# Four fused blocks on one core: a quad's reciprocal and scaling written behind the mask addition of the quad two further on

## The chip, the core and the metric

The kernel runs on one core of a Trainium2 chip. Its time is the device time of one execution in microseconds, the median of several runs; lower is better. The engines are called by the profile's names: PE (TensorE, matmuls), PEld (its weight loads), DVE (VectorE), ACT (ScalarE), POOL (GpSimd) and SP (SyncE, which issues nearly all DMAs). All arithmetic is float32.

## What is computed

An image batch `x` of 4 x 56 x 56 x 256 goes through four residual blocks, each `x = x + block(groupnorm(x))`:

- layer 0: attention in a 7 x 7 window around every pixel, 8 heads of 32 channels, keys and values padded with zeros at the border
- layer 1: every image's 3136 tokens against each other: `A = exp(5 * cosine)` without its diagonal, normalised by rows, then `rowsum * (xW + b) - (A x) W`, layer norm, leaky ReLU
- layer 2: neighbourhood attention with a 7 x 7 window clamped at the border and a position bias; half of the heads use a dilation of 2
- layer 3: attention inside shifted 7 x 7 windows, with a position bias and a mask

The part that the change touches is the softmax of layers 0, 2 and 3, cut to its core:

```python
logits = q @ k + bias_or_mask
attn = softmax(logits)              # exp(l) / sum(exp(l))
out = attn @ v                      # here: (exp(l) @ v) * (1 / sum(exp(l)))
x = x + out @ w_o + b_o
```

## The kernel before, in words

`direct_blocks` computes everything without subtracting a maximum before the exponential. At its end a flag tells whether any sum became too large; only then a second program, `fused_blocks`, computes all again. It did not run here.

In layers 0, 2 and 3 the work is a stream of **quads**. A quad is four heads times one tile of queries (112 in layer 0, 98 in layer 2, four pairs of windows of 98 in layer 3) with all keys that these queries see. Two quads (eight heads) make up a tile in layers 0 and 2, and a row of windows in layer 3. There are 224, 256 and 64 quads.

`attend_quads` (L932) runs the stream. For each quad:

1. `logits` (L941): PE multiplies keys by queries (L948) into two PSUM tiles of two banks, `s0` and `s1`, one buffer each. For the first half DVE adds the mask into SBUF tile `e0` (L954) and ACT takes the exponential in place (L955). For the second half ACT takes the exponential straight from PSUM (L957) and POOL multiplies by the exponential of the mask (L958).
2. `fill`: the steps of other work dealt out to this quad by `spread`: projections of the next rows (L901 with their evictions by ACT, values at L918 with L920 on DVE), the output projection of the row before (L901 on `attn`), normalisation (L895), statistics (L872), loads.
3. `products` of the quad before this one (`held`): PE multiplies the exponentials by the values and by ones (L967) into `ps_o`: numerators and sums. Then its `done` step: in layers 0 and 2 after every second quad, in layer 3 after each, `finish` takes the reciprocal of the sums into tile `rs` (L1091 or L1093 and L1096 in layer 0, L1416 in layer 2, L1633 in layer 3), POOL adds `rs` to a running sum (`seen`, L926), and DVE scales the numerators into `attn` (L1098, L1422, L1635). That makes 112 + 128 + 64 = 304 finishes.

`ps_o` has two buffers in layers 0 and 2 (one for a pair of quads) and a single one of two banks in layer 3. The output projection of row r - 1 reads `attn` and is dealt out within row r: in layer 3 it is the first step of the second quad's fill.

What decides the order on an engine: the Python source records operations in the order in which it runs. The framework then builds one list per engine. It takes an operation when the operations that it needs are ready by its own reckoning and its buffers are free, and among those that are ready it takes the one recorded first. Semaphore waits are put in afterwards. The built list of an engine can so differ from the source. In DVE's list of the kernel before, 277 of the 304 finishes have the mask addition of the quad two further on between reciprocal and scaling, although the source has it behind both.

Of the kernel before, what the change touches and what calls it, by code (L numbers as in the profile page):

```python
# [814 lines left out]
def direct_blocks(ctx: ExitStack, tc: tile.TileContext, d: dict, watch):  # L815
# [7 lines left out]
    no_step = lambda: None  # L823
# [27 lines left out]
    def psum_tile(tag, bufs, banks=1):  # L851
        shape = [P, 512] if banks == 1 else [P, banks, 512]
        return ps.tile(shape, FP, tag=tag, name="ps_" + tag, bufs=bufs)
# [78 lines left out]
    def attend_quads(pool, units):  # L932

        def logits(w):  # L941
            nk, nq, nu = w["nk"], w["nq"], len(w["pieces"])
            w["first"]()
            w["e"] = []
            s = [psum_tile(f"s{a}", 1, 2) for a in range(2)]
            for u, (k, q, *_) in enumerate(w["pieces"]):
                for j in range(4):
                    nc.tensor.matmul(s[j // 2][:nk, j % 2, u * nq:(u + 1) * nq], lhsT=k(j), rhs=q(j),  # L948
                                     start=True, stop=True)
            for a in range(2):  # L950
                e = pool.tile([P, 2, w["width"]], FP, tag=f"e{a}", name=f"e{a}", bufs=2)
                ev, sv = e[:nk, :, :nu * nq], s[a][:nk, :, :nu * nq]
                if a == 0:
                    nc.vector.tensor_tensor(ev, sv, w["mask"].to_broadcast([nk, 2, nu * nq]), ALU.add)  # L954
                    nc.scalar.activation(ev, ev, AF.Exp)  # L955
                else:
                    nc.scalar.activation(ev, sv, AF.Exp, accum_out=w.get("sum"))  # L957
                    nc.gpsimd.tensor_tensor(ev, ev, w["emask"].to_broadcast([nk, 2, nu * nq]), ALU.mult)  # L958
                w["e"].append(e)

        def products(w):
            nk, nq = w["nk"], w["nq"]
            for k in range(2):
                for u, (_, _, v, start, stop) in enumerate(w["pieces"]):
                    po = w["o"](k, u)
                    for j in range(4):
                        nc.tensor.matmul(  # L967
                            po[j * HD:(j + 1) * HD], lhsT=ones[:nk, :HD] if k else v(j),
                            rhs=w["e"][j // 2][:nk, j % 2, u * nq:(u + 1) * nq], start=start, stop=stop)
            w["done"]()  # L970

        held = None
        for w in units:
            logits(w)
            w["fill"]()
            if held:
                products(held)
            held = w
        products(held)

    def spread(units, steps):

        n = len(units)
        for i, w in enumerate(units):
            mine = steps[i * len(steps) // n:(i + 1) * len(steps) // n]
            w["fill"] = lambda mine=mine: [f() for f in mine]
            yield w
# [11 lines left out]
    def layer0(big, pool):  # L999
# [151 lines left out]
        for r in range(3):  # L1151
            prepare(r)
            if r < 2:
                for step in project_rows(r):
                    step()
        attend_quads(pool, stream())
        for step in project_out(NIMG * NCH - 1):
            step()
# [186 lines left out]
    def layer2(big, pool):  # L1345
# [153 lines left out]
        for i in range(3):  # L1499
            prepare(i + 1)  # L1500
            for step in project_rows(i):
                step()
        attend_quads(pool, stream())
        for step in project_out(NIMG * NSB - 1):
            step()
# [61 lines left out]
    def layer3(big, pool):  # L1567
# [108 lines left out]
        for step in project_rows(0):  # L1676
            step()
        attend_quads(pool, stream())
        for step in project_out(NIMG * 8 - 1):
            step()  # L1680
# [74 lines left out]
def _build(arrays):  # L1755
    import concourse.bacc as bacc

    nc = bacc.Bacc("TRN2", target_bir_lowering=False, num_devices=1)
    d = {n: nc.dram_tensor("in_" + n, a.shape, mybir.dt.from_np(a.dtype), kind="ExternalInput").ap()
         for n, a in arrays.items()}  # L1760
    d["out"] = nc.dram_tensor("out_x", (NIMG, C, T), FP, kind="ExternalOutput").ap()
    with tile.TileContext(nc) as tc:
        with tc.tile_pool(name="flag", bufs=1) as pool:
            flag = pool.tile([1, 1], I32, name="flag")
            with tc.tile_pool(name="watch", bufs=1) as wp:
                watch = [wp.tile([P, n], FP, name=f"watch{n}") for n in (WC, 2 * CC + 2, 4 * NIMG * 8)]
                for w in watch:
                    nc.vector.memset(w, 0.0)
                direct_blocks(tc, d, watch)
                unsafe(tc, wp, watch, flag)  # L1770
            again = nc.values_load(flag)
            with tc.If(again > 0):
                fused_blocks(tc, d)
    return nc
# [10 lines left out]
```

## Time and profile before

| what | value |
|---|---|
| median of 3 runs | 4694.75 us (4692.59 to 4698.1) |
| the profiled execution, as a run | 4702.85 us |
| its span, first to last instruction | 4701.1 us |
| mean granted PE clock | 0.973 |
| DVE: reciprocals L1416, L1633, L1096, L1091 busy | 176.5, 166.5, 111.5, 62.2 us |
| mean of one of them | 1379, 2602, 1549, 1556 ns |
| DVE: mask addition L954, layers 0, 2, 3 busy | 152.1, 146.2, 58.6 us |
| mean of one of them | 679, 571, 915 ns |
| DVE: scaling L1422, L1098, L1635 busy | 52.7, 42.6, 35.4 us |

The profile is of one execution. Times are counted from the span's start. A row of the timeline has the start, the busy time, the engine, the line, the operation with its output and inputs and how many were merged, and in brackets how long the engine sat idle before it and what ended that. A row of busy time by stretch has the stretch and its length, then the busy time and count of PE, PEld, DVE, ACT and POOL, the granted PE clock, the DMA engines' busy share and GB/s. A row of the waits has who waited for whom, the total in microseconds, how often, and the longest.

Layer 0 takes roughly the stretch from 65 to 935 us, layer 1 from 935 to 3150, layer 2 from 3150 to 4000 and layer 3 from 4000 to the end. The change does not touch layer 1.

### The profile page before, as it was taken

Reading aid. Unit: us, or ns where it says so; the run is one execution under the profiler, and the core shown is the slowest. Engines: PE = TensorE matmul, PEld = TensorE weight load, DVE = VectorE, ACT = ScalarE, POOL = GpSimd, SP = SyncE. Lnnn points to the kernel's source line nnn. Section 1 sums busy time; section 2 is a strip of 40 time slices with the busy share of each in tenths; the row PEclk is TensorE's granted clock in tenths of the full one; section 3 lists DMA queues with packets and bytes.
Section 4 is the critical chain, followed back from the end, with each engine's and each line's share of the span. In section 5 each row is a group of like instructions: output and inputs, shape, how many; then the busy total and the mean of one; then the engine's idle time right before and its main releaser. Section 6 shows DMA issues by size and latency. Waiting matters only on the chain.

```text
span 4701.1 us, 104255 instructions
## 1 busy us (share of the span) xinstructions
PE 4340.8 (92%) x44910; PEld 2896.0 (62%) x44910; DVE 2384.5 (51%) x4745; ACT 1369.8 (29%) x2750; POOL 1458.5 (31%) x1835
## 2 busy tenths in 40 slices
PE   6989999899999999999999999969999998888887
PEld 4756666566665666666666666646666665555554
DVE  5566666633444333443434433445666666555655
ACT  2234444411111111111111111114444444333332
POOL 2234444411124111231123211224344444333333
PEclk9799999999999999999999999989999999999999
DMA  5243333210000000010000000033333333211211
GB/s 196 72 123 105 118 102 94 86 40 9 22 17 25 13 20 15 17 33 8 22 13 17 16 8 9 16 113 90 101 99 98 100 100 113 63 56 55 61 56 43
DMA packets 237208, 277.91 MB, mean 59 GB/s; under 512 B 20270, under 2 KB 229088, under 8 KB 236000
## 3 DMA queue, kind: packets, MB, share of 16 engines
q1 hardware_dynamic: 236306, 270.30, 18.8%
q8 instruction: 354, 5.80, 0.5%
q14 instruction: 116, 0.95, 0.1%
q10 hardware_dynamic: 432, 0.86, 0.0%
HBM read 191.58 MB, written 79.53 MB: 58 GB/s over the span
## 4 chain that ended last, share of the span: by engine, by line
PE 72%; DVE 12%; POOL 6%; issue 5%; DMA 3%; ACT 1%; SPq 0%; DVEq 0%; POOLq 0%; ACTq 0%
PE ps_m L901 14%; PE ps_o L1266 11%; PE ps_o L967 9%; PE ps_s L1231 9%; PE ps_v L1258 9%; PE ps_m L918 7%; PE ps_s L948 5%; PE ps_t L1249 2%; DVE e L954 2%; POOL y L1299 2%; POOL y L1300 2%; PE ps_m L1204 2%; DMA x<-in_x 1%; DVE xn L895 1%; POOL rstd L1297 1%
## 5 line engine op out<-in xcount | busy, mean ns | idle before, releaser
L1262 DVE TENSOR_TENSOR acc<-acc,ps_v 128x257 f32<-128x257 f32 x1104 | 458.3, 420 | 773.8 <-PE ps_v L1258 769.8
L1266 PE MATMUL ps_o<-xw,at 128*128 128x257 f32 (+1 forms) x2400 | 664.9, 394 | 1.1 <-DVE at L908 0.8
L1234 ACT ACTIVATE e<-ps_s 128x512 f32<-128x512 f32 (+5 forms) x364 | 195.3, 537 | 1592.4 <-PE ps_s L1231 1559.8
L1258 PE MATMUL ps_v<-xw,e 128*128 128x257 f32 (+1 forms) x2400 | 647.4, 385 | 6.2 <-DVE acc L1260 6.2
L1231 PE MATMUL ps_s<-xnT,xd 128*128 128x512 f32 (+4 forms) x1456 | 628.2, 546 | 0.0
L957 ACT ACTIVATE e<-ps_s 119x392 f32<-119x392 f32 (+7 forms) x544 | 324.6, 597 | 754.8 <-PE ps_s L948 738.6
L1266 PEld LDWEIGHTS ps_o<-xw,at 128*128 128x128 f32 (+1 forms) x2400 | 422.0, 189 | 165.7 <-ACT at L910 56.8
L926 POOL TENSOR_TENSOR watch<-watch,rs 128x196 f32<-128x196 f32 (+2 forms) x304 | 215.7, 710 | 985.8 <-DVE rs L1633 396.3
L1258 PEld LDWEIGHTS ps_v<-xw,e 128*128 128x128 f32 (+1 forms) x2400 | 407.4, 186 | 105.8 <-DVE acc L1262 31.1
L955 ACT ACTIVATE e<-e 119x392 f32<-119x392 f32 (+7 forms) x544 | 343.1, 631 | 418.7 <-DVE e L954 404.6
L901 PE MATMUL ps_m<-xn,w_wqkv 128*128 128x392 f32 x1024 | 395.4, 518 | 30.5 <-DVE xn L895 30.5
L1227 POOL TENSOR_SCALAR xd<-xnT,vec 128x128 f32<-128x128 f32 (+1 forms) x200 | 121.5, 619 | 851.6 <-PE ps_s L1231 842.3
L958 POOL TENSOR_TENSOR e<-e,m0t 119x448 f32<-119x448 f32 (+3 forms) x224 | 294.9, 1317 | 227.5 <-ACT e L957 226.7
L967 PE MATMUL ps_o<-e,ones 100*32 100x112 f32 (+7 forms) x10752 | 360.4, 256 | 0.0
L1231 PEld LDWEIGHTS ps_s<-xnT,xd 128*128 128x128 f32 x1456 | 254.3, 189 | 167.2 <-issue 149.1
L967 PEld LDWEIGHTS ps_o<-e,vp 119*32 119x32 f32 (+4 forms) x8704 | 193.3, 111 | 237.9 <-issue 159.2
L958 POOL TENSOR_TENSOR e<-e,bias 119x392 f32<-119x392 f32 (+3 forms) x256 | 259.1, 1012 | 232.6 <-ACT e L957 232.3
L918 PE MATMUL ps_m<-w_wqkv,xn 128*98 128x256 f32 x1024 | 259.4, 398 | 65.2 <-ACT k L1610 41.6
L967 PE MATMUL ps_o<-e,vp 119*32 119x98 f32 (+6 forms) x8704 | 310.8, 263 | 4.8 <-POOL e L958 4.1
L920 DVE TENSOR_TENSOR v<-ps_m,bc 98x512 f32<-98x512 f32 (+1 forms) x184 | 126.4, 687 | 359.5 <-PE ps_m L918 246.9
L967 PEld LDWEIGHTS ps_o<-e,ones 100*32 100x32 f32 (+5 forms) x10752 | 278.4, 112 | 7.3 <-issue 7.3
L901 PEld LDWEIGHTS ps_m<-xn,w_wqkv 128*128 128x128 f32 x1024 | 184.1, 193 | 142.6 <-issue 20.7
(137 smaller groups left out, 5932.1 us busy)
## 6 DMA issues: line engine op xcount, KB each, us to landing
x<-in_x SPq DMA_DIRECT2D x56, 448.0 KB
x<-xr SPq DMA_DIRECT2D x56, 448.0 KB
x<-x SPq DMA_DIRECT2D x60, 392.0 KB
xr<-x SPq DMA_DIRECT2D x60, 392.0 KB
vp<-vd SPq DMA_DIRECT2D x224, 59.5 KB
xr<-in_x SPq DMA_DIRECT2D x28, 448.0 KB
vd<-v SPq DMA_DIRECT2D x28, 448.0 KB
xr<-x SPq DMA_DIRECT2D x28, 448.0 KB
```

The costliest lines, as they stand in the source:

```text
L901: nc.tensor.matmul(pm[:, :n], lhsT=w[:, h, col:col + P], rhs=rhs(h), start=(h == 0), stop=(h == CC - 1))
L918: nc.tensor.matmul(pm[:n, j * C:(j + 1) * C], lhsT=xn[:, h, k * n:(k + 1) * n], rhs=w[:, h, :], start=(h == 0), stop=(h == CC - 1))
L926: nc.gpsimd.tensor_tensor(w, w, rs, ALU.add)
L948: nc.tensor.matmul(s[j // 2][:nk, j % 2, u * nq:(u + 1) * nq], lhsT=k(j), rhs=q(j), start=True, stop=True)
L955: nc.scalar.activation(ev, ev, AF.Exp)
L957: nc.scalar.activation(ev, sv, AF.Exp, accum_out=w.get("sum"))
L958: nc.gpsimd.tensor_tensor(ev, ev, w["emask"].to_broadcast([nk, 2, nu * nq]), ALU.mult)
L967: nc.tensor.matmul(po[j * HD:(j + 1) * HD], lhsT=ones[:nk, :HD] if k else v(j), rhs=w["e"][j // 2][:nk, j % 2, u * nq:(u + 1) * nq], start ...
L1231: nc.tensor.matmul(s[:nj, :n], lhsT=xd[j][:, h, :nj], rhs=xnT[:, h, first * P:first * P + n], start=(h == 0), stop=(h == CC - 1))
L1258: nc.tensor.matmul(pv[:ni, :C + 1], lhsT=e[:nj, col(i)], rhs=xw[:nj, j, :], start=True, stop=True)
L1262: nc.vector.tensor_tensor(acc[:ni, i, :], acc[:ni, i, :], pv[:ni, :C + 1], ALU.add)
L1266: nc.tensor.matmul(out[j][:nj, :C + 1], lhsT=e[:nj, col(i)] if i == j else at[:size(i), tcol(i)], rhs=xw[:size(i), i, :], start=(i == j), ...
```

## The change

The `done` step of a quad is no longer called at the end of `products`. The loop keeps it and calls it in the next turn, behind `logits` of the next quad in line and ahead of that quad's fill. After the last quad the two steps still open are called. Nothing else changes: no operation, no buffer and no shape. From the first changed line on, lines of the kernel after are numbered 1 higher (inside `logits` and `products`) or 4 higher (below the loop).

```diff
@@ -967,16 +968,19 @@
                         nc.tensor.matmul(
                             po[j * HD:(j + 1) * HD], lhsT=ones[:nk, :HD] if k else v(j),
                             rhs=w["e"][j // 2][:nk, j % 2, u * nq:(u + 1) * nq], start=start, stop=stop)
-            w["done"]()
-
-        held = None
+
+        held, done = None, no_step
         for w in units:
             logits(w)
+            done()
             w["fill"]()
             if held:
                 products(held)
+                done = held["done"]
             held = w
+        done()
         products(held)
+        held["done"]()
```

## The prediction

> **What bounds the kernel now.** I read the page first, then busy time by stretch, then the waits, then the timeline at the places that the change reaches. The page:
>
> ```profile
> PE 4340.8 (92%) x44910; PEld 2896.0 (62%) x44910; DVE 2384.5 (51%) x4745; ACT 1369.8 (29%) x2750; POOL 1458.5 (31%) x1835
> ...
> PE 72%; DVE 12%; POOL 6%; issue 5%; DMA 3%; ACT 1%; SPq 0%; DVEq 0%; POOLq 0%; ACTq 0%
> ```
>
> TensorE is busy or first in the chain nearly everywhere; VectorE (DVE), which the change re-sorts, has 12% of the chain. Busy time by stretch; the three rows are layers 0, 2 and 3:
>
> ```profile
> 65.00:935.00 870.00, 827.48 (x13906) 558.59 (x13902) 551.34 (x826) 366.27 (x710) 366.04 (x341) 0.94 0.33 98
> ...
> 3150.00:4000.00 850.00, 807.47 (x14730) 532.73 (x14729) 510.70 (x927) 381.59 (x832) 334.29 (x392) 0.98 0.34 101
> 4000.00:4701.10 701.10, 588.07 (x7437) 375.06 (x7436) 387.51 (x528) 219.24 (x384) 263.74 (x326) 0.97 0.18 54
> ```
>
> PE (first figure after the length) is idle 42.5, 42.5 and 113.0 us. In layer 3 the waits give part of it to the step that the change wants ahead:
>
> ```profile
> PE ps_s L948 <- DVE e L954: 38.0, 31, 1.2
> ```
>
> So logits wait 38.0 us for the previous mask addition (L954) to free the score buffer; the same line reads 26.7 in layer 0 and 10.9 in layer 2. The reason seems to be the reciprocal ahead of it. An ordinary layer 3 row:
>
> ```profile
> 4208.34 0.95 PE L948 MATMUL ps_s<-q,k 32*98 32x98 f32 x32
> 4208.55 2.61 DVE L1633 RECIPROCAL rs<-ps_o 128x392 f32<-128x392 f32 x1
> ...
> 4211.07 0.91 DVE L954 TENSOR_TENSOR e<-ps_s,m3l 98x784 f32<-98x784 f32 x1
> ...
> 4211.90 0.55 DVE L1635 SCALAR_TENSOR_TENSOR attn<-ps_o,rs 128x392 f32<-128x392 f32 x1
> ...
> 4212.52 1.58 PE L901 MATMUL ps_m<-attn,w_wp 128*128 128x392 f32 x4
> ```
>
> The source of before writes reciprocal, scaling, mask addition. The chip ran reciprocal, **mask addition**, scaling. The list is sorted by readiness, and source order only breaks ties.
>
> **What the Trainium skill says.** "PSUM — Partial Sum Buffer", section "Engine vs sequencer instructions": VectorE, ScalarE and GpSimd work strictly first in, first out, and matmuls start and complete in program order. So what counts is the built list, not the source. The trace agrees: at 4211.07 the mask addition starts 1.78 us after its logits ended (4209.29), behind the reciprocal. "VectorE: DVE Perf Modes", section "First, the fixed hardware budget": a reciprocal is an iterative division with a repeat count of 8. The trace agrees that it is dear: 2.61 us against 0.55 for the scaling of the same 128x392. This is what a mask addition would be spared.
>
> **The change, part by part.** It adds and removes no arithmetic, so its price is in order, waits and addresses. I compared the built lists of both kernels, engine by engine, line numbers shifted to match.
>
> 1. VectorE: 304 pairs of reciprocal and scaling (112 + 128 + 64). Before, in 277 the mask addition stands between the two (91, 127, 59), in 27 none does. After, 281 have it between (92, 127, 62). In none does it stand ahead of the reciprocal, in either kernel. So the list differs in four swaps of neighbours: one in layer 0, three in layer 3, once at the start of images 1 to 3.
> 2. TensorE: four matmuls (eight passes) of the products move ahead of a value projection at those three places; nothing else. ScalarE: at the same places the exponential (L955) moves ahead of the key eviction (L1610).
> 3. GpSimd and SP: same operations in the same order, so every DMA is issued from its old place. In layer 3 the rs and xr tiles get swapped addresses.
>
> The layer 3 place, seen at image 1:
>
> ```profile
> 4150.57 0.94 PE L948 MATMUL ps_s<-q,k 32*98 32x98 f32 x30
> ...
> 4153.29 3.81 DVE L895 TENSOR_SCALAR xn<-x,gst 128x343 f32<-128x343 f32 x6
> ...
> 4156.47 5.56 PE L901 MATMUL ps_m<-xn,w_wqkv 128*128 128x392 f32 x8 [4.96 <-DVE xn L895]
> 4157.02 0.55 DVE L1635 SCALAR_TENSOR_TENSOR attn<-ps_o,rs 128x392 f32<-128x392 f32 x1
> ...
> 4157.51 0.96 DVE L954 TENSOR_TENSOR e<-ps_s,m3l 98x784 f32<-98x784 f32 x1
> ...
> 4160.76 0.59 ACT L1610 ACTIVATE k<-ps_m,vec 128x392 f32<-128x392 f32 x1 [8.20 <-PE ps_m L901]
> 4161.25 0.85 ACT L955 ACTIVATE e<-e 98x784 f32<-98x784 f32 x1
> 4161.96 0.51 PE L967 MATMUL ps_o<-e,v 98*32 98x98 f32 x2
> ```
>
> What is late is the normalisation; PE waits 4.96 us for it, and the swap stands behind it. Swapped, the mask addition starts at 4157.02, 0.49 earlier, and ends near 4157.93; the scaling then ends near 4157.93 + 0.55 + 0.08 = 4158.6, some 1.0 later. The scaling's reader is the first product (the output buffer is single in layer 3), at 4161.96: 3.4 us of cover, given by eight key and query matmuls. Without that cover it would cost 1.0. The exponential gets idle ScalarE time near 4158 (its 8.20 idle) and stops standing between two evictions. PE waited 0.26 for L955 before the value projection; the four products moved there fill that. Gain 0 to 0.26 at each of three, none if the clock or the next eviction takes it: 0 to -0.8. Against: if the cover failed everywhere, 3 x 1.0 = +3.0.
>
> Layer 0's place:
>
> ```profile
> 256.83 0.63 DVE L872 BATCH_NORM_STATS2 st<-x 128x6 f32<-128x448 f32 x1 [5.69 <-DMA x<-in_x]
> 257.37 0.38 DVE L1098 TENSOR_TENSOR attn<-ps_o,rs 128x224 f32<-128x224 f32 x1
> 257.66 0.85 DVE L954 TENSOR_TENSOR e<-ps_s,m0t 100x672 f32<-100x672 f32 x1
> ...
> 258.57 1.15 PE L948 MATMUL ps_s<-q,kE 32*119 32x112 f32 x16 [3.87 <-DVE e L954]
> ```
>
> PE stood still for this mask addition, itself behind a statistic that waits for a DMA. Swapped it starts 0.29 earlier, and so do the logits: 0 to -0.3. The low end counts because the chain goes back to the next x<-in_x transfer 1.4 us later, which does not move. The scaling's reader is an output projection several quads on.
>
> Addresses: both rs buffers are used in turn already, and the 64 reciprocals in layer 3 span only 2587 to 2609 ns, their 64 GpSimd readers 1010 to 1039. If every one went to its extreme it would be 64 x 0.03 = 2 us, on engines with slack; I take 0.
>
> Sum: bounds -1.1 and +3.0; I take -0.5. The profiled execution spans 4701.1 us (4702.85 as a run), so its like would span 4700.6. That run lies 8.1 us above the median of three, 4694.75, from which I forecast 4694.3.
>
> **Rivals.**
> - A, faster: the mask addition really goes ahead of the reciprocal. Then at most the PE waits of layers 0 and 2 vanish, 26.7 + 10.9 = 37.6 us: 4657. For it: those waits and the row above. Against: the list has no such case.
> - B, slower: the same in layer 3, where the scaling is the next thing needed. Mask addition 4209.29 to 4210.20, reciprocal to 4212.81, scaling to 4213.44; the output projection that now starts at 4212.52 would start 0.9 later. In 31 rows: +28 us, 4723. It decides from about ten rows on (10 x 0.9 = 9). Against it: the list again, and the earlier release of the scores.
> - C: the change does not do what it says. That is my forecast: four swaps of 304.
> - D: the cover of step 1 fails, +3.0: 4698, still no difference.
>
> **How the numbers follow.** About 0.2%, 9.4 us, is what a measurement of this kernel can tell from no change. Forecast, C: 0.91, with D's 0.04 inside "same"; A 0.02; B 0.03. Range: the three runs span 5.5 us and another median may sit as far off: 4694.3 - 5.5 = 4688.8, and with D above, 4694.3 + 5.5 + 3.0 = 4702.8, about where the profiled run lies. I write 4688.5 to 4702.5. A and B stay outside, with 0.05.
>
> **What would show it.** Right: layers 0, 2 and 3 as long as before within 2 us each; L954 still between L1633 and L1635 in ordinary rows; the 38.0 us wait still there; at the start of images 1 to 3 L954 ahead of L1635 and L955 ahead of L1610, with PE's 4.96 unchanged. Wrong: L954 ahead of L1633 (A, B), L901 waiting longer for L1635 (B), or products waiting for L1635 at those three places (D). Also wrong: a shift in all layers, which no part here can make.

## The result, and the profile after

The changed kernel takes 4698.55 us (median of 4 runs, 4692.99 to 4703.24), beside 4696.43 us of the kernel before on the same chip (4 runs, 4692.59 to 4702.7). The ratio is 1.0003, with a 95% interval of 0.9985 to 1.002: no difference. The profiled execution spans 4697.9 us (4699.74 as a run); that of before spanned 4701.1.

The page of the kernel after, busy time and the chain's shares by engine:

```profile
PE 4334.9 (92%) x44910; PEld 2891.5 (62%) x44910; DVE 2383.9 (51%) x4745; ACT 1371.5 (29%) x2750; POOL 1460.8 (31%) x1835
...
PE 72%; DVE 12%; POOL 6%; issue 5%; DMA 3%; ACT 1%; SPq 0%; DVEq 0%; POOLq 0%; ACTq 0%
```

The same instructions, the same shares, digit for digit in the chain. Measured from the last output addition of one layer to that of the next (layer 3 then begins at 3980.8 us and not at the rough 4000 of the table of stretches), layers 0 to 3 took 933.6, 2189.4, 857.8 and 720.3 us before, and 932.3, 2187.9, 857.5 and 720.2 after. Layer 1, which has no part in the change, moved by 1.5 us; that is as much as any.

The waits of the kernel after from 4000 us to the end (who waited for whom, total us, how often, longest):

```profile
PE ps_m L918 <- ACT k L1614: 41.6, 28, 2.4
PE ps_s L949 <- DVE e L955: 38.0, 31, 1.2
```

The 38.0 us of logits waiting for the mask addition are untouched. The 41.6 us above it, which the prediction did not look at, become the subject of the experiments. An ordinary layer 3 row of the timeline of after:

```profile
4163.62 0.95 PE L949 MATMUL ps_s<-q,k 32*98 32x98 f32 x32
4163.75 2.61 DVE L1637 RECIPROCAL rs<-ps_o 128x392 f32<-128x392 f32 x1
...
4166.27 0.91 DVE L955 TENSOR_TENSOR e<-ps_s,m3l 98x784 f32<-98x784 f32 x1
...
4167.10 0.55 DVE L1639 SCALAR_TENSOR_TENSOR attn<-ps_o,rs 128x392 f32<-128x392 f32 x1
```

Reciprocal, mask addition, scaling: the order of before. The edit is in the source and not in the list. The start of image 1, one of the three places in layer 3 where the list does differ:

```profile
4154.32 4.38 PE L901 MATMUL ps_m<-xn,w_wqkv 128*128 128x392 f32 x8 [4.96 <-DVE xn L895]
...
4154.88 0.96 DVE L955 TENSOR_TENSOR e<-ps_s,m3l 98x784 f32<-98x784 f32 x1
...
4155.76 0.55 DVE L1639 SCALAR_TENSOR_TENSOR attn<-ps_o,rs 128x392 f32<-128x392 f32 x1
4155.87 0.86 ACT L956 ACTIVATE e<-e 98x784 f32<-98x784 f32 x1 [5.45 <-DVE e L955]
...
4158.08 0.59 ACT L1614 ACTIVATE k<-ps_m,vec 128x392 f32<-128x392 f32 x1 [1.35 <-PE ps_m L901]
...
4158.63 0.53 PE L968 MATMUL ps_o<-e,v 98*32 98x98 f32 x10
```

Mask addition ahead of scaling, exponential ahead of key eviction, and the first products 2.3 us behind the scaling's end, with no wait for it. Below, a *pass* is one PE instruction of the profile; the eight passes (x8) at 4154.32 are the key and query matmuls. From their start, the mask addition comes at 0.56 (1.04 before), the scaling at 1.44 (0.55 before).

### The profile page after: what moved, and what is told of

Its sections match the earlier page's. It is cut to its first block, busy times and chain, and to the rows that moved or that the text cites. A ratio compares the mean times of both kernels' runs of the same rounds, so it can differ in the third digit from the quotient of the medians.

```text
span 4697.9 us, 104254 instructions
## 1 busy us (share of the span) xinstructions
PE 4334.9 (92%) x44910; PEld 2891.5 (62%) x44910; DVE 2383.9 (51%) x4745; ACT 1371.5 (29%) x2750; POOL 1460.8 (31%) x1835
## 4 chain that ended last, share of the span: by engine, by line
PE 72%; DVE 12%; POOL 6%; issue 5%; DMA 3%; ACT 1%; SPq 0%; DVEq 0%; POOLq 0%; ACTq 0%
PE ps_m L901 14%; PE ps_o L1270 11%; PE ps_s L1235 9%; PE ps_o L968 9%; PE ps_v L1262 9%; PE ps_m L918 7%; PE ps_s L949 5%; PE ps_t L1253 2%; DVE e L955 2%; DMA x<-in_x 2%; POOL y L1303 2%; POOL y L1304 2%; PE ps_m L1208 2%; DVE xn L895 1%; POOL rstd L1301 1%
## 5 line engine op out<-in xcount | busy, mean ns | idle before, releaser
L1270 PEld LDWEIGHTS ps_o<-xw,at 128*128 128x128 f32 (+1 forms) x2400 | 422.0, 189 | 165.6 <-ACT at L910 56.7
L918 PE MATMUL ps_m<-w_wqkv,xn 128*98 128x256 f32 x1024 | 257.5, 396 | 65.3 <-ACT k L1614 41.6
```

Of the source, the lines that this page charges most:

```text
L918: nc.tensor.matmul(pm[:n, j * C:(j + 1) * C], lhsT=xn[:, h, k * n:(k + 1) * n], rhs=w[:, h, :], start=(h == 0), stop=(h == CC - 1))
L1270: nc.tensor.matmul(out[j][:nj, :C + 1], lhsT=e[:nj, col(i)] if i == j else at[:size(i), tcol(i)], rhs=xw[:size(i), i, :], start=(i == j), ...
```

## The experiments

Every difference below is against the kernel before, run on the same chip: its median is 4697.76 us beside the first four kernels, 4694.37 beside `late_projection`, `mask_02_scale_3`, `late_projection_mask_3` and `late_mask_02_scale_3`, and 4697.11 beside the other four. A ratio and its interval rest on all runs, so a ratio can differ a little from the quotient of two medians. Lengths of layers, waits, idle and busy times come from one profiled run of each kernel, and that of before, 4702.85 us, lies some us above its medians. They repeat only within some us: in the profiles of the seven kernels that have layer 0 as in before or after, it takes 926.3 to 933.6 us.

To bind an order that the source does not enforce, this helper was used. It adds no wait and no instruction; it only tells the list builder to take one operation behind another:

```python
def behind(op, other):
    if other is not None:
        info = mybir.DependencyInfo(mybir.DependencyClass.NoSync, mybir.DependencyReason.SCHED_ONLY)
        tc.add_manual_dep(op.ins, other.ins.name, info, reason="order")
```

One caution holds for all these runs but `key_first`: the builder reacts to an edit, so other lists change with the one that is meant. In the traces PE's order differs from before in each of them, and ACT's in several, `scale_first` and `late_projection` among them. `key_first` changes ACT's order alone.

### Mask addition really ahead, layers 0 and 2 (rival A)

On the kernel after; the `done` step gets the mask addition of the quad just emitted, and the reciprocal is bound behind it:

```diff
-                    nc.vector.tensor_tensor(ev, sv, w["mask"].to_broadcast([nk, 2, nu * nq]), ALU.add)
+                    w["added"] = nc.vector.tensor_tensor(ev, sv, w["mask"].to_broadcast([nk, 2, nu * nq]), ALU.add)
...
-            done()
+            done(w["added"])
...
-                nc.vector.reciprocal(rs, pv[:, :, 1, :])
+                behind(nc.vector.reciprocal(rs, pv[:, :, 1, :]), after)
```

> The kernel after, with the order that its source asks for made binding in layers 0 and 2: the reciprocal may not be listed ahead of the mask addition of the quad two further on. It then stands behind it in 111 and 127 of the finishes (none before). My theory (the kernel after does not move because its list does not move, while PE's waits for the mask addition are real): the waits of logits for L954 in layers 0 and 2, 26.7 + 10.9 us, shrink to a few us, and the time falls by 20 to 38 us, to 4660 to 4676; scaling comes later, but its reader is several quads away. Rival (the order on VectorE does not matter, because another wait ends in its place): within 9 us of 4696.

Measured: 4661.17 us, ratio 0.9925 (0.9912 to 0.9938), 36.6 us less than before. Layers 0 and 2 are 23.8 and 13.1 us shorter, layer 3 is as before. This is rival A's size, and it answers what the edit would have been worth, had it reached the list, together with what the builder changed in PE's list along with it (a dozen places in layer 0, some thirty in layer 2). The layers' parts are less firm than the total: in the four kernels below that bind the same order here, layer 0 is 18.7 to 29.0 us shorter. And it is not quite the account that A gave. In layer 2, PE's wait for the mask addition falls from 11.9 to 2.4 us (the layer taken in full), as A has it. In layer 0, PE's own waits read, before:

```profile
PE ps_s L948 <- DVE e L954: 26.7, 22, 3.9
...
PE ps_m L901 <- DVE attn L1098: 3.6, 3, 2.6
```

and with the mask addition first:

```profile
PE ps_s L954 <- DVE e L960: 20.8, 13, 5.6
PE ps_m L901 <- DVE attn L1107: 9.4, 8, 2.9
```

Only 5.9 us of the first wait are gone, and the wait for the scaling has grown by 5.8. What shrank is PE's whole idle time between 65 us and the layer's end (868.6 - 827.1 = 41.5, then 844.8 - 814.5 = 30.3) and its busy time (12.6 us less, at a granted clock of 0.95 instead of 0.94). Of A's 37.6 us, 15.4 are found in the waits that it named (5.9 and 9.5); that the total fits is in part luck. Why the same matmuls were busy for less time is not settled; some us of it can be the spread of layer 0 from run to run.

### The same in layer 3 (rival B)

The same edit with only `behind(nc.vector.reciprocal(rs, box["o"][:, 1, :WC]), after)`; 62 of 64 finishes then have the mask addition ahead.

> The kernel after, with the order binding in layer 3 alone (62 of 64 finishes). My theory: the output projection of the row before waits for the scaling, which comes 0.9 us later in each of 31 rows: +28 us, to about 4724, less what the earlier release of the score buffer gives back. Rival (the 38.0 us in which PE waits for L954 are the larger part): faster by up to 38 us. Rival (cover): within 9 us of 4696.

Measured: 4691.13 us, ratio 0.9993 (0.9985 to 1.0001): no difference is shown, though layer 3 is 4.4 us shorter in the profile. B's +28 did not come. Its mechanism did, and dearer. PE's own waits of this kernel in layer 3:

```profile
PE ps_m L901 <- DVE attn L1644: 57.7, 32, 2.2
...
PE ps_m L918 <- ACT k L1619: 2.4, 1, 2.4
```

The output projection now waits 57.7 us for the scaling, 1.8 each time. In return the 38.0 us for L954 are no longer in the list and the 41.6 us for the key eviction shrink to 2.4. PE's idle time falls from 130.8 to 103.0 us. Yet its busy time rises from 589.5 to 612.9. Groups of PE's instructions by form, in layer 3 (count, busy us, mean ns of one, idle before), of before:

```profile
L901 PE MATMUL ps_m<-attn,w_wp 128*128 128x392 f32 x256 | 103.3, 527 | 3.4 <-DVE attn L1635 1.3
```

and of this kernel:

```profile
L901 PE MATMUL ps_m<-attn,w_wp 128*128 128x392 f32 x256 | 124.1, 616 | 57.7 <-DVE attn L1644 57.7
```

The same 256 passes take 20.8 us more. One row shows a reason; the timeline, then busy time by stretch (length, busy time and count of PE, PEld, DVE, ACT, POOL, granted clock, DMA share, GB/s):

```profile
4202.42 2.53 PE L901 MATMUL ps_m<-attn,w_wp 128*128 128x392 f32 x4 [1.87 <-DVE attn L1644]
```

```profile
4197.00:4202.40 5.40, 3.55 (x84) 2.31 (x72) 4.42 (x5) 1.77 (x3) 2.35 (x2) 1.00 0.08 29
4202.40:4204.90 2.50, 2.48 (x5) 0.92 (x5) 0.00 (x0) 0.59 (x1) 0.98 (x2) 0.60 0.00 0
```

The four passes take 2.53 us instead of 1.58, because the clock is 0.60 behind a stall of 1.87 us. Over the layer it is 0.90, before 0.96. So B's term was 0.9 for each row, and the row paid 1.8 in waiting and about 0.65 (20.8 / 32) in clock. B counted from 4212.52, where the second half of the projection started before; but PE had stood 1.24 us for the mask addition until 4212.04 (shown below, under the later output projection). Without that wait PE is done with its logits near 4210.80 + 0.95 = 4211.75 (an estimate from the same row), 1.7 us ahead of the scaling's end at 4213.44. On the other side B named the earlier release of the score buffer without pricing it, and did not see the key eviction.

### Scaling ahead of the mask addition

On the kernel before: `behind(<mask addition>, <last scaling emitted>)` in all three layers, so that no mask addition stands between reciprocal and scaling.

> The kernel before, with its own source order made binding: the mask addition may not be listed ahead of the scaling of the finish recorded before it. Then no mask addition stands between reciprocal and scaling any more (277 before), in all three layers. My theory: mask additions come later by one scaling, 0.38 us in layer 0, 0.49 in layer 2, 0.63 in layer 3. Where PE waited for them it waits longer: 22 x 0.38 + 19 x 0.49 + 31 x 0.63 = 37 us; in layer 3 the output projection gets the scaling 0.9 us earlier, which gives back up to 28. Sum +10 to +37, to 4706 to 4733. Rival (the order does not matter): within 9 us of 4696.

Measured: 4683.37 us, ratio 0.9969 (0.9958 to 0.9981), 14.4 us less, where the theory had 10 to 37 more. In the profile layers 0 and 2 are 7.6 and 14.9 us longer, with the expected sign; layer 3 is 22.7 us shorter, which no theory had. These parts add up to 1.5 us less (layer 1 included) and not to 14.4: the six runs go from 4673.02 to 4701.47 us while the granted clock goes from 0.975 to 0.968, and the profile is of the longest. PE's own waits in layer 3:

```profile
PE ps_m L901 <- DVE attn L1642: 50.8, 32, 1.7
PE ps_m L901 <- DVE xn L895: 31.3, 4, 16.1
PE ps_m L901 <- ACT q L1621: 14.8, 27, 0.6
...
PE ps_m L918 <- ACT k L1617: 2.4, 1, 2.4
```

Again the key eviction's 41.6 and L954's 38.0 are gone against a new wait for the scaling. DVE's orders in these two kernels are opposite, so no one order of DVE accounts for both. ACT's queue may: in `mask_first_3` the exponential has its input early, and in this kernel ACT's list, re-sorted in passing, takes the key eviction ahead of the exponential in 30 rows. `key_first` below tests it.

### No reciprocal

On the kernel before, all four reciprocals become `nc.vector.tensor_scalar_mul(..., 1 / 2401)`. This leaves the division by the sum out of the computation; only the time is read.

> The kernel before, with each of the 304 reciprocals replaced by a multiplication by 1/2401 of the same operands, so that the output is not the reference's: it shows what the length of the reciprocal costs at all. VectorE loses some 2 us per finish in layer 3 (2.60 to about 0.6) and 1.1 in layers 0 and 2 (1.4 to 1.55, to about 0.35), 400 us of its busy time. My theory: PE's waits for L954 (75.6 us in the three layers) nearly vanish, and in layer 3 the scaling comes 2 us earlier: 60 to 110 us faster, 4586 to 4636. Rival (VectorE's order and length are off the path): within 20 us of 4696.

Measured: 4524.12 us, ratio 0.9631 (0.9619 to 0.9644), 173.6 us less; layers 0, 2 and 3 are 37.3, 31.3 and 116.2 us shorter. The upper end of the expectation, 110, was too small. But the length of the reciprocal is not all that changed. With shorter operations to reckon with, the builder made other lists: in this trace a mask addition stands between the two operations of a finish in 1 of 304 (277 before), and no output projection of layer 3 is cut in two by logits any more (30 were). So 173.6 us are what the length and these lists bring together, though DVE was only 51% busy. What the length alone costs is not shown, nor is 173.6 us shown to be a bound for what other orders can bring: `late_mask_02_scale_3` below comes within 27 us of it with every reciprocal in place.

### Key eviction ahead of the exponential (the 41.6 us)

An ordinary row of before, in the timeline:

```profile
4221.96 0.91 DVE L954 TENSOR_TENSOR e<-ps_s,m3l 98x784 f32<-98x784 f32 x1
...
4222.90 0.86 ACT L955 ACTIVATE e<-e 98x784 f32<-98x784 f32 x1 [1.86 <-DVE e L954]
...
4223.67 0.57 ACT L1610 ACTIVATE k<-ps_m,vec 128x392 f32<-128x392 f32 x1
4224.14 0.58 ACT L1614 ACTIVATE q<-ps_m,qbias 128x392 f32<-128x392 f32 x1
4224.29 1.97 PE L918 MATMUL ps_m<-w_wqkv,xn 128*98 128x256 f32 x8 [1.47 <-ACT k L1610]
```

ACT stands 1.86 us idle in front of an exponential that waits for the mask addition, which stood behind the reciprocal. The key eviction, whose matmuls are done, is queued behind that exponential, and PE needs its PSUM buffer for the values. On the kernel before, in layer 3 only, the exponential L955 is bound behind the key eviction of the same quad's fill (`latest` is emptied ahead of the layer; here the helper tests its first argument, so nothing is bound while `latest` is empty):

```diff
-                    nc.scalar.activation(ev, ev, AF.Exp)
+                    latest[0] = nc.scalar.activation(ev, ev, AF.Exp)
...
-                nc.scalar.activation(kT[:, m, :], pm, AF.Identity, bias=bk3[:, m:m + 1])
+                behind(latest[0], nc.scalar.activation(kT[:, m, :], pm, AF.Identity, bias=bk3[:, m:m + 1]))
```

PE, DVE, POOL and SP take their operations in the order of before, also in the traces; only ACT's differs.

> The kernel before, with one order bound in layer 3: the exponential L955 may start only behind the key eviction L1610 of the same quad. In the built lists ScalarE's is the only one that changes. Theory K (the value projection's wait for the key eviction comes from ScalarE's list: the eviction stands behind an exponential that waits for a mask addition, which waits for the reciprocal): the 41.6 us of ps_m L918 waiting for ACT k L1610 go, and so does most of the 38.0 us of logits waiting for L954 if the two were one wait seen twice; layer 3 is 25 to 45 us shorter, about 4660. Rival (PE is short of work in this layer anyway, and the next wait, the scaling or the logits, takes the place): within 10 us of before.

Measured: 4648.25 us, ratio 0.9892 (0.9875 to 0.9908), 48.9 us less; layer 3 is 50.7 us shorter, more than the 25 to 45 expected. Theory K holds for the 41.6 us; that the 38.0 us were the same wait seen twice does not. The same form of line as above, PE's values in layer 3, before and then in this kernel:

```profile
L918 PE MATMUL ps_m<-w_wqkv,xn 128*98 128x256 f32 x512 | 125.1, 388 | 41.6 <-ACT k L1610 41.6
```

```profile
L918 PE MATMUL ps_m<-w_wqkv,xn 128*98 128x256 f32 x512 | 121.2, 379 | 0.0
```

The waits of this kernel in layer 3 (here 3978 to 4648 us) still hold the other line:

```profile
PE ps_s L955 <- DVE e L961: 38.0, 31, 1.2
```

So the two waits were separate, and nothing took the place of the first. Of the 50.7 us, 42.1 are PE's idle time (130.8 to 88.7) and 8.6 its busy time.

### A later output projection (the 38.0 us)

In before, PE's list takes the first half of the output projection (the part that reads the row's first quad) as soon as it can. That opens both `ps_m` buffers, and the second half, which reads the quad just finished, has to come behind its scaling. In 30 rows PE's list puts two passes of the next quad's logits between the halves, and there they wait for L954. PE in an ordinary row of before:

```profile
4209.22 1.58 PE L901 MATMUL ps_m<-attn,w_wp 128*128 128x392 f32 x4
4212.04 0.41 PE L948 MATMUL ps_s<-q,k 32*98 32x98 f32 x2 [1.24 <-DVE e L954]
4212.52 1.58 PE L901 MATMUL ps_m<-attn,w_wp 128*128 128x392 f32 x4
```

On the kernel before, in layer 3:

```diff
-                    i = len(steps) // 2 + 1
-                    steps[i:i] = project_out(r - 1)
+                    steps += project_out(r - 1)
```

> The kernel before, with the two output projection steps of layer 3 dealt out behind the query and value steps of the second quad instead of ahead of them; VectorE's order is left to itself, mask addition between reciprocal and scaling as before. Theory S (layer 3 is bound where the output projection waits for the scaling): the 11.4 us in which PE waits for L1635 go, -11, to about 4686; the 38.0 us for L954 stay. Rival P (scale_first gained because PE's list got more regular: 977 changes between logits, projections and products in layers 2 and 3 against 1097; here 971): -20 to -25, to about 4674. Rival (nothing of that binds): within 9 us of 4697.

Measured: 4637.68 us, ratio 0.9875 (0.986 to 0.989), 56.7 us less, more than either theory gave; layer 3 is 60.8 us shorter. Theory S started from a mixed figure: of its 11.4 us, 10.1 are waits of the weight loads (PEld) and 1.3 PE's own. PE's own waits of this kernel in layer 3:

```profile
PE ps_m L918 <- ACT k L1610: 37.4, 28, 2.4
PE ps_m L901 <- ACT q L1614: 28.1, 33, 0.9
...
PE ps_s L948 <- DVE e L954: 2.7, 1, 2.7
```

The 38.0 us are 2.7, with the reciprocal still ahead of the mask addition (the latter stands between reciprocal and scaling in 62 of 64 finishes) and no logits between the halves any more: the reciprocal alone did not make that wait. 28.1 us for the query eviction are new. PE's idle time falls by 27.2 us and its busy time by 33.6. Most of the second lies in runs that are no longer cut in two: 12.7 in the logits (94 runs in PE's order, then 64), 16.5 in the products (99 runs, then 66). The logits by form, before and then here:

```profile
L948 PE MATMUL ps_s<-q,k 32*98 32x98 f32 x2048 | 74.2, 257 | 39.1 <-DVE e L954 38.0 <-ACT e L957 1.1
```

```profile
L948 PE MATMUL ps_s<-q,k 32*98 32x98 f32 x2048 | 61.5, 256 | 2.7 <-DVE e L954 2.7
```

The mean of one is the same, 257 and 256 ns, and the sum is 12.7 us less: within a run the passes overlap, 32 of them take 0.95 us together, and a run cut in two pays more. In the row above, the two passes that stand alone at 4212.04 take 0.41 us; 30 in one run take 0.94 (at 4150.57 in the prediction), so that the cut costs some 0.4 us. Times 30 rows this is 12 us, an estimate that fits.

### Combinations

`mask_02_scale_3` joins the mask addition ahead in layers 0 and 2 and the scaling ahead in layer 3.

> The binding order of mask_first_02 in layers 0 and 2 and that of scale_first in layer 3, together. In their profiles layer 0 was 23.8 us shorter and layer 2 13.1 us (mask addition first), layer 3 22.7 us (scaling first). Theory: each layer is bound on its own, so the parts add up: -59.6, to about 4638. Rival (the gain of layer 3 in scale_first came with its slower layer 2, or from PE's clock of that run): 4655 to 4662.

Measured: 4634.37 us, 0.987 (0.9854 to 0.9885), 60.0 us less, as the sum has it (36.6 + 22.7 = 59.3). The parts fit less well: in this kernel's own profile layers 0, 2 and 3 are 25.6, 10.4 and 31.2 us shorter. PE's idle time in layer 3 is that of `scale_first` (118.6 and 117.9 us), its busy time is not (570.5 and 579.7), so the 22.7 of that profile were too little, and the match of the sums is in part luck.

`late_projection_mask_3` joins the later projection and the mask addition ahead in layer 3.

> mask_first_3 with the same later place of the output projection in layer 3. In mask_first_3 PE waits 57.7 us for the scaling in 32 waits of 1.8 us, the price of my rival B, and what it gained on the score buffer was lost there. Theory: with 3.4 us of query and value matmuls ahead of the output projection the scaling is hidden: those 57.7 us go, to about 4635 to 4645. Rival (the wait moves: PE then waits as long for the mask addition or an eviction): within 10 us of mask_first_3, 4681 to 4701.

Measured: 4588.05 us, 0.9767 (0.9754 to 0.978), 106.3 us less. With the projection out of the way, nothing reads the scaling soon, and the price that `mask_first_3` paid is gone: layer 3 takes 610.8 us instead of its 715.9. That is nearly twice what the theory had: PE's idle time falls by 54.0 us, as forecast, and its busy time by another 51.1, with the granted clock of the layer back from 0.90 to 0.96.

`late_projection_key` joins the later projection and the key eviction ahead of the exponential.

> late_projection with the key eviction bound ahead of the exponential in layer 3 as well. Theory K: the 37.4 us of L918 waiting for ACT k L1610 that late_projection still has go: 4600 to 4612. If they are hidden by the 28.1 us of L901 waiting for ACT q, less than 15 us come off: above 4622.

Measured: 4591.82 us, 0.9776 (0.976 to 0.9792), 105.3 us less: 56.7 + 48.9 = 105.6. The two gains in layer 3 add up. This is 8 us better than theory K's range; the waits for the query eviction hid nothing, 27.2 of their 28.1 us are still there. It is also level with the run above, which has the two waits down in another way: there the exponential has its input early.

`late_mask_02_scale_3` adds the later projection to `mask_02_scale_3`; the last two join the parts differently.

> mask_02_scale_3 with the later output projection in layer 3. Theory: in layer 3 the scaling comes first already, so the later place hides what is left of PE's wait for it (50.8 us in 32 waits in scale_first): 30 to 50 us below mask_02_scale_3. Rival (the mask addition, now behind reciprocal and scaling, ends last): within 10 us of mask_02_scale_3.

> Mask addition ahead of the reciprocal in layers 0 and 2, late projection and key eviction ahead of the exponential in layer 3. Additive: late_projection_key less 36.6, near 4565 to 4575; level with late_mask_02_scale_3 (4547.85) only if the order of the key eviction is all that the scaling's order brought there.

> Mask addition ahead of the reciprocal in all three layers, late projection in layer 3. Additive: late_projection_mask_3 (4588.05) less the 36.6 of layers 0 and 2: 4551, level with late_mask_02_scale_3 within 8 us.

Measured: 4547.85 us (0.9679, 0.9665 to 0.9692), 4555.02 us (0.9694, 0.9678 to 0.9711) and 4554.02 us (0.9697, 0.9681 to 0.9713). The intervals overlap: three ways to the same 3.0 to 3.2%. The first is 86.5 us below `mask_02_scale_3`, where 30 to 50 were expected; in layer 3, PE's idle time fell by 65.9 us and its busy time by 23.0. The second is again a sum, 105.3 + 36.6 = 141.9 against 142.1 measured; the expectation, 4565 to 4575, had its first part too small. The third came out as expected.

## Why the prediction was right

- **The list decides.** The forecast was C: the edit does not do what it says. It rested on the built lists, and the trace has them: reciprocal, mask addition, scaling in ordinary rows, layers within 1.5 us. `mask_first_02` shows that this and not the edit's idea was the reason for no gain in layers 0 and 2: bound into the list, the same order brings 36.6 us (with the changes in PE's list that came along). In layer 3 the idea itself would have brought nothing that can be told, as `mask_first_3` shows. "PSUM — Partial Sum Buffer", section "Engine vs sequencer instructions" of the Trainium skill, which the prediction took for first in, first out, is borne out by `key_first`, where ACT's order alone moved 48.9 us: a ready eviction was not taken ahead of a waiting exponential.
- **Step 1, layer 3.** Predicted: mask addition 0.49 earlier, scaling some 1.0 later, inside 3.4 us of cover. Measured: 0.48, 0.89, and no wait. Predicted gain 0 to 0.26 at each place: none can be seen. The 0.26 was misread in any case: it is a wait of the weight loads (PEld) at 4162.40, while PE itself was busy until 4162.47. (The addition was also reckoned at 0.91 us where its own line reads 0.96; that changes nothing.) From the start of the key matmuls to the next reciprocal, the eight passes themselves taken off, images 1 to 3 took 5.20, 5.05 and 5.05 us before and 5.05, 5.04 and 5.34 after. The eight passes vary by more than that (see the end), so 0.26 at each place could not have been seen.
- **Step 1, layer 0.** Predicted: logits 0.29 earlier behind the statistic. Measured from the statistic's start: 1.74 us before, 1.44 after, as these lines of after show:

```profile
257.41 0.63 DVE L872 BATCH_NORM_STATS2 st<-x 128x6 f32<-128x448 f32 x1 [5.23 <-DMA x<-in_x]
...
258.85 0.74 PE L949 MATMUL ps_s<-q,kE 32*119 32x112 f32 x16 [3.10 <-DVE e L955]
```

  The layer's length does not show it: 1.3 us less, where layer 1 alone moved by 1.5.
- **Addresses, GpSimd and SP** at nothing: POOL's order and SP's order of DMAs are as before, POOL's busy time moved by 2.3 us of 1458.5; nothing points to a cost.
- **The sum.** -0.5 was predicted. The medians measured side by side differ by +2.1 us, with an interval of about -7 to +9: sign and size are below what can be told.
- **The rivals.** A had its size right, 37.6 against 36.6, though the waits that it added up shrank by 15.4 only. B named a wait that is real, at half of what it turned out to cost (0.9 for each row against 1.8), left the release of the score buffer unpriced, and did not see the 41.6 us for the key eviction, which went as well. D did not come.
- **A reason that was half right.** The prediction gave the reciprocal ahead of the mask addition as the reason of the 38.0 us. `mask_first_3` takes them away by putting the mask addition first, while logits still stand between the halves of the projection in 30 rows. `late_projection` takes away all but 2.7 with the reciprocal still first, because no logits stand between the halves any more; nor do they in `scale_first`, where the mask addition comes later still and the wait is gone too. So the wait needs both. `no_reciprocal` can't decide it, since both are gone there.

## What to carry to other kernels

When a framework sorts operations, compare the built lists before costing an edit of the source: if they are the same, the edit can bring next to nothing, and the idea behind it has to be bound into the list to be tested. When an in-order engine stands idle before an instruction, look at what is queued behind that one: here a key eviction, ready but behind an exponential, cost 48.9 us on an engine that was 29% busy over the whole kernel. And a wait priced alone can mislead in both directions, as in layer 3, where binding the order added 57.7 us of one wait and still came out level.

## What was not expected of the hardware

A short stall of PE costs more than its length. Behind the 4.96 us stall at the start of images 1 to 3 the eight key and query passes took 5.56, 5.00 and 4.58 us before, and 4.38, 4.27 and 5.57 after, against 2.90 for the same eight in an ordinary row. Stretches of after around image 1:

```profile
4154.30:4158.70 4.40, 4.38 (x12) 2.29 (x16) 3.60 (x12) 1.45 (x2) 0.00 (x0) 0.65 0.34 91
4158.70:4162.00 3.30, 3.30 (x23) 2.23 (x22) 0.00 (x0) 0.59 (x1) 0.00 (x0) 1.00 0.50 122
```

The clock granted is 0.65, then full. "TensorE: Matmul & The Clock Gate", section "HAM oscillation — how this bites in real kernels" of the Trainium skill, gives the rule of no idle gaps above about 3.4 us. The 4.96 us agree with it. The 1.87 us stall in `mask_first_3`, with 0.60 behind it, does not fit it: here shorter gaps slowed PE as well, but not each time. Two rows of `scale_first`, 21 us apart, have the same stall; the timeline, then the 4 us behind it:

```profile
4120.67 3.94 PE L901 MATMUL ps_m<-attn,w_wp 128*128 128x392 f32 x6 [1.67 <-DVE attn L1642]
...
4141.66 2.24 PE L901 MATMUL ps_m<-attn,w_wp 128*128 128x392 f32 x6 [1.67 <-DVE attn L1642]
```

```profile
4120.60:4124.60 4.00, 3.93 (x7) 2.18 (x8) 0.90 (x3) 1.33 (x2) 3.64 (x5) 0.57 0.00 0
...
4141.60:4145.60 4.00, 3.94 (x13) 2.42 (x14) 0.90 (x2) 2.24 (x4) 4.00 (x6) 1.00 0.00 0
```

In layer 3 the granted clock fell within 4 us behind 20 of the 26 stalls of 1.8 to 2.0 us in `mask_first_3`, behind 9 of the 27 of 1.6 to 1.8 us in `scale_first` and 6 of 28 such in `mask_02_scale_3`, and behind none of the 22 of 1.4 to 1.6 us in before. What decides between two equal stalls is not shown.
